# Another cut of one output stream into store slots (pairwise products, one core)

## The chip, the cores and the metric

One core of a Trainium2 chip runs the whole kernel. The metric is the device time of one execution in microseconds (us); the time of a kernel is the median of its runs.

## The reference, cut to what matters

```python
def _L0_rec_ref(x, W):                          # x (4096, 32, 64), W (64, 64), float32
    vid = jnp.einsum('bfd,de->bfe', x, W)
    idx_i, idx_j = jnp.triu_indices(32, k=1)    # 496 pairs i < j
    return x[:, idx_i, :] * vid[:, idx_j, :]    # (4096, 496, 64)
```

Each of 4096 samples has 32 fields of 64 numbers. The fields are multiplied by one 64x64 matrix, and for each of the 496 pairs (i, j) the field i is multiplied, element by element, with the transformed field j. The input has 33.6 MB, the output 520.1 MB.

## The kernel before, in words

**Layout.** The 128 partitions hold two halves of the batch times the 64 embedding numbers. The batch of one half is cut into 16 tiles of C = 128 samples. A **unit** is one field or one pair of one tile: 128 partitions by 128 float32, 64 KB. A tile has 32 units of input and 496 units of output; the program writes 16 * 496 = 7936 units of output, in one long row. The host brings the arrays into this layout and back.

**Memory.** The SBUF tile `mem` has 445 units. Everything lies in it: the inputs of the tiles (at `XPLACE`) and the products that wait to be stored. PSUM holds `vid`, the 32 transformed fields of one tile.

**Work on one tile.** TensorE multiplies the tile with the matrix into `vid` (L173, in pieces of 4 fields). VectorE then forms the products (L197): one `tensor_tensor` multiplies several left fields with several right fields and writes a run of units (112 at most) that lie one behind the other in the output. `by_block` gives the order of the runs. Left operands come from `mem`, right ones from PSUM.

**Slots.** The row of 7936 output units is cut into slots by the list `SLOTS`. A slot is (number of units, place in `mem`, seams...). At most 127 units are in a slot. When the products of a slot are done, one DMA stores it (L200). `STARTS` are the ends of the slots in the output row; `BREAKS` are these ends and the seams inside the slots. The function `products` splits a run of products wherever a break lies in it, so every break inside a run costs more VectorE instructions. A seam is put where the place of a slot crosses the edge of an older slot whose store may still be on its way: the products ahead of the seam need not wait for that store.

**What waits for what.** A product waits for the matmuls of its right fields, for the load of its tile, and for every older store (or load) whose place in `mem` it writes over. A matmul waits until VectorE has read the old contents of its part of `vid`. A store waits for the products of its slot. The first store behind a group of loads also waits until the last but one piece of these loads has landed (`behind`). All DMAs are issued by SP and go through one queue.

**Order.** Only SP keeps the order of the program text (`manual_schedule` with SP alone). The order of the instructions on VectorE and TensorE is set when the kernel is built, by the scheduler of the framework; it mostly follows the text, but it may put a ready product ahead of others. Loads are three groups: tile 0 to 5 at the start, tiles 6 to 10 at about 382 us, tiles 11 to 15 at about 790 us (L152).

Of the kernel before, what the change touches and what calls it, by code (L numbers as in the profile page):

```python
# [26 lines left out]


SLOTS = [
    (108, 80), (116, 201), (96, 64, 16), (96, 161, 40), (60, 257), (108, 64, 97), (92, 172),  # L30
    (84, 265), (127, 80, 92), (127, 222, 43), (98, 64, 16), (92, 162, 60), (127, 254), (120, 64),
    (124, 184, 70), (104, 308), (124, 112, 72), (124, 240), (124, 64, 48), (124, 192, 48),
    (124, 317), (124, 152, 40), (96, 64, 88), (124, 161), (112, 32, 32), (85, 144, 17), (56, 229),
    (104, 48), (116, 160, 69), (127, 1, 47), (72, 128, 32), (85, 200), (124, 32), (127, 160, 40),
    (85, 0, 32), (118, 85, 75), (114, 203), (127, 32, 53), (127, 159, 44), (123, 0, 32),
    (123, 123, 36), (127, 246), (112, 0), (127, 119), (126, 246), (127, 160, 86), (124, 289),
    (88, 160), (81, 248, 41), (84, 329), (104, 160, 88), (92, 264, 65), (88, 357), (127, 176, 88),
    (127, 318, 39), (127, 136, 40), (127, 272, 46), (94, 128), (106, 222, 50), (116, 328),
    (127, 160, 62), (127, 288, 40), (127, 120, 40), (127, 247, 41), (127, 64, 56), (124, 191, 56),
    (124, 317), (127, 32), (127, 160), (124, 289), (103, 136, 24),  # L40
]


# [210 lines left out]
```

## Time and profile before

| | |
|---|---|
| median of 3 runs | 1288.05 us (1287.6 to 1288.36) |
| the profiled execution | 1287.84 us, of which the span from the first to the last instruction is 1286.1 us |
| moved by DMA | 553.79 MB, mean 431 GB/s over the span |
| VectorE busy | 1091.1 us, 456 instructions |
| TensorE busy | 223.2 us, 512 matmuls in the trace |
| stores | 71, of at most 127 units (8128 KB) |

The page gives the busy time of each engine, the span in 40 slices, the DMA queues, the chain of work that ended last, the groups of instructions with their mean durations, and the DMA issues with the time from issue to landing. "SPq" is the queue of SP: the time that its next DMA stood waiting. Beside the page the trace has the record of each DMA packet (start, duration, size) and of each instruction.

### The profile page before, as it was taken

Reading aid. Unit: us, or ns where it says so; the run is one execution under the profiler, and the core shown is the slowest. Engines: PE = TensorE matmul, PEld = TensorE weight load, DVE = VectorE, ACT = ScalarE, POOL = GpSimd, SP = SyncE. Lnnn points to the kernel's source line nnn. Section 1 sums busy time; section 2 is a strip of 40 time slices with the busy share of each in tenths; the row PEclk is TensorE's granted clock in tenths of the full one; section 3 lists DMA queues with packets and bytes.
Section 4 is the critical chain, followed back from the end, with each engine's and each line's share of the span. In section 5 each row is a group of like instructions: output and inputs, shape, how many; then the busy total and the mean of one; then the engine's idle time right before and its main releaser. Section 6 shows DMA issues by size and latency. Waiting matters only on the chain.

```text
span 1286.1 us, 1762 instructions
## 1 busy us (share of the span) xinstructions
PE 223.2 (17%) x512; PEld 41.0 (3%) x512; DVE 1091.1 (85%) x456; POOL 0.2 (0%) x4
## 2 busy tenths in 40 slices
PE   4031221303120113030311311103131130312000
PEld 1000000000000000000000000000000000000000
DVE  6899889988995489998998995649999799999952
POOL 0000000000000000000000000000000000000000
PEclk8565555555555655555555555555555565656555
DMA  9999999999999999999999999999999999999998
GB/s 415 434 422 429 434 447 425 437 433 440 415 440 419 445 426 427 436 423 435 444 432 424 442 422 445 421 423 434 436 441 431 421 437 433 441 431 433 428 441 380
DMA packets 11817, 553.79 MB, mean 431 GB/s; under 512 B 1312, under 2 KB 1312, under 8 KB 1696
## 3 DMA queue, kind: packets, MB, share of 16 engines
q1 hardware_dynamic: 11808, 553.69, 99.8%
q8 instruction: 4, 0.07, 0.0%
q14 instruction: 5, 0.04, 0.0%
HBM read 33.59 MB, written 520.09 MB: 431 GB/s over the span
## 4 chain that ended last, share of the span: by engine, by line
DMA 51%; DVE 44%; issue 3%; PE 0%; DVEq 0%; SPq 0%
DVE mem L197 44%; DMA out_dram<-mem 44%; DMA mem<-in_r_x_dram 7%; PE vid L173 0%; DVEq L242 0%; SPq L152 0%; SPq L200 0%; DVEq L197 0%; DVE w L142 0%
## 5 line engine op out<-in xcount | busy, mean ns | idle before, releaser
L197 DVE TENSOR_TENSOR mem<-mem,vid 128x1024 f32<-128x1024 f32 (+16 forms) x455 | 1090.9, 2471 | 164.9 <-DMA out_dram<-mem 154.8
L173 PE MATMUL vid<-mem,w 64*64 64x512 f32 x512 | 223.2, 996 | 961.0 <-DVE mem L197 863.5
L173 PEld LDWEIGHTS vid<-mem,w 64*64 64x64 f32 x512 | 41.0, 198 | 1141.6 <-DVE mem L197 1007.7
L142 DVE COPY w<-mem 128x64 f32<-128x64 f32 x1 | 0.2, 195 | 5.8 <-DMA mem<-in_r_x_dram 5.8
L222 POOL MEMSET const-uint8-127<- 128x1 uint8 x1 | 0.1, 102 | 0.0
L222 POOL MEMSET const-bfloat16-1.0<- 128x1 bf16 x1 | 0.1, 101 | 0.0
L222 POOL MEMSET const-float32-0.0<- 128x1 f32 x1 | 0.1, 98 | 0.2 <-issue 0.2
L222 POOL MEMSET const-float32-1.0<- 128x1 f32 x1 | 0.1, 98 | 0.0
## 6 DMA issues: line engine op xcount, KB each, us to landing
out_dram<-mem SPq DMA_DIRECT2D x21, 8128.0 KB, 26.7
out_dram<-mem SPq DMA_DIRECT2D x13, 7936.0 KB, 28.2
out_dram<-mem SPq DMA_DIRECT2D x3, 7424.0 KB, 24.2
out_dram<-mem SPq DMA_DIRECT2D x3, 6656.0 KB, 22.7
out_dram<-mem SPq DMA_DIRECT2D x3, 6144.0 KB, 20.9
out_dram<-mem SPq DMA_DIRECT2D x3, 5888.0 KB, 23.9
out_dram<-mem SPq DMA_DIRECT2D x3, 5440.0 KB, 24.6
mem<-in_r_x_dram SPq DMA_DIRECT2D x2, 8128.0 KB, 39.2
```

Source lines behind the costliest of these rows:

```text
L142: nc.vector.tensor_copy(w2, mem[:, place - 1, C - D :])
L173: nc.tensor.matmul(vid[half, b : b + BANK, :], lhsT=w2[half, :], rhs=xt[half, b : b + BANK, :], start=True, stop=True,)
L197: nc.vector.tensor_tensor(o, left, right, ALU.mult)
L222: nc = _bacc.Bacc("TRN2", target_bir_lowering=False, num_devices=1, dynamic_dma_scratch_size=1024)
```

## The change

The list `SLOTS` is another one. Nothing else is changed.

```diff
 SLOTS = [
-    (108, 80), (116, 201), (96, 64, 16), (96, 161, 40), (60, 257), (108, 64, 97), (92, 172),
-    (84, 265), (127, 80, 92), (127, 222, 43), (98, 64, 16), (92, 162, 60), (127, 254), (120, 64),
-    (124, 184, 70), (104, 308), (124, 112, 72), (124, 240), (124, 64, 48), (124, 192, 48),
-    (124, 317), (124, 152, 40), (96, 64, 88), (124, 161), (112, 32, 32), (85, 144, 17), (56, 229),
-    (104, 48), (116, 160, 69), (127, 1, 47), (72, 128, 32), (85, 200), (124, 32), (127, 160, 40),
-    (85, 0, 32), (118, 85, 75), (114, 203), (127, 32, 53), (127, 159, 44), (123, 0, 32),
-    (123, 123, 36), (127, 246), (112, 0), (127, 119), (126, 246), (127, 160, 86), (124, 289),
-    (88, 160), (81, 248, 41), (84, 329), (104, 160, 88), (92, 264, 65), (88, 357), (127, 176, 88),
-    (127, 318, 39), (127, 136, 40), (127, 272, 46), (94, 128), (106, 222, 50), (116, 328),
-    (127, 160, 62), (127, 288, 40), (127, 120, 40), (127, 247, 41), (127, 64, 56), (124, 191, 56),
-    (124, 317), (127, 32), (127, 160), (124, 289), (103, 136, 24),
+    (96, 221), (120, 80), (116, 200, 21), (100, 64, 16), (92, 164, 36), (92, 256), (127, 96, 68),
+    (124, 223, 33), (125, 64), (120, 191), (64, 311), (112, 79), (124, 224), (108, 64),
+    (120, 176, 48), (112, 301), (120, 64), (112, 205), (120, 320), (112, 93), (127, 205), (121, 64),
+    (96, 189), (120, 48), (116, 168, 21), (100, 32), (104, 132, 36), (48, 236), (124, 16),
+    (127, 157, 79), (109, 0, 16), (120, 109, 48), (88, 229), (127, 16, 93), (127, 160, 69),
+    (114, 0, 16), (120, 114), (112, 237), (127, 0), (121, 128), (120, 261), (127, 1), (127, 128),
+    (122, 259), (120, 176), (116, 297), (92, 160, 16), (88, 252, 45), (72, 341), (120, 160, 92),
+    (120, 293, 48), (32, 413), (120, 173), (126, 319), (122, 144), (127, 287, 32), (119, 128, 16),
+    (126, 247), (127, 96), (109, 223), (112, 333), (127, 158), (127, 285), (127, 64, 94),
+    (127, 192, 93), (124, 320), (120, 48), (127, 190), (124, 317), (125, 158),
 ]
```

There are 70 slots with 22 seams in place of 71 with 41, and VectorE has 345 products in place of 455. The list is one line shorter, so L197 of before is L196 of the changed kernel, and so on.

As built, the changed kernel has its VectorE products in the order of the program text, but for two of them. One of 4 units stands four places early (in the slot (92, 160, 16)). The other is one of 80 units of the slot (127, 64, 94), which stands five places early. This is the part of the built order with it; "n units at p" is a product of n units that is written to place p of `mem`, and the slot that it belongs to stands behind it:

```
96 at 236                                          (109, 223)   waits for the store of (126, 247)
112 at 333                                         (112, 333)
16 at 158, 8 at 174, 8 at 182, 8 at 190, 16 at 198 (127, 158)   the first waits for the store of (127, 96)
16 at 214, 48 at 230, 7 at 278                     (127, 158)   the first waits for the store of (109, 223)
1 at 285, 8 at 286, 8 at 294, 8 at 302, 8 at 310   (127, 285)
80 at 66                                           (127, 64, 94)   <- in the text behind the next five
16 at 318, 16 at 334, 56 at 350, 6 at 406          (127, 285)   the first waits for the store of (112, 333)
2 at 64, 12 at 146, ...                            (127, 64, 94)
```

In the kernel before, products stand ahead of their place in the text too, eleven groups of them, the largest product among them of 16 units.

## The prediction

> **What bounds the kernel now.** I read the page from its totals downward. First the busy times beside the DMA rows:
>
> ```profile
> PE 223.2 (17%) x512; PEld 41.0 (3%) x512; DVE 1091.1 (85%) x456; POOL 0.2 (0%) x4
> DMA  9999999999999999999999999999999999999998
> DMA packets 11817, 553.79 MB, mean 431 GB/s; under 512 B 1312, under 2 KB 1312, under 8 KB 1696
> q1 hardware_dynamic: 11808, 553.69, 99.8%
> ```
>
> The 16 DMA engines are busy for 99.8% of the span, in every slice; VectorE for 85%. So the kernel is a stream of DMA, and its time is the bytes by the rate, plus the start, plus every microsecond in which the DMA engines have nothing to do. The packet records agree: from the first store on, all 16 engines have a packet in flight practically always. The bytes are the same after the change, so it can gain next to nothing from VectorE's time. The question is only whether a store comes too late.
>
> Then the waits, VectorE's and SP's own:
>
> ```profile
> DVE mem L197 <- DMA out_dram<-mem: 154.8, 34, 22.7
> SPq L200 <- DVE mem L197: 1100.8, 66, 33.6
> ```
>
> It is a ring. VectorE waits for room in `mem` (34 times, until a store has landed); SP waits for VectorE before 66 of its stores. The memory is so full that hardly more than one finished store stands behind the running one. How much is in hand is read from the chain of waits, whose DMA pieces run from a store's issue to its landing:
>
> ```profile
> 588.41 23.26 DMA out_dram<-mem
> ...
> 1053.72 24.57 DMA out_dram<-mem
> ...
> 1129.96 26.09 DMA out_dram<-mem
> ```
>
> The first and third are stores of 127 units, the second one of 116. By the packet records 127 units alone take 19.2 us and 116 units 17.6 us, so these stood some 4 to 7 us, landing included. The records of the first packets give the cover itself, issue to first packet: 2.0 us for the store at 588.41 (the smallest inside a group of tiles), 4.6 to 7 us for most. A store issued to idle engines (at 30.70) needs 0.84 us to its first packet. So cover beyond 0.84 us is what VectorE may be late.
>
> [...]
>
> **The price of a product.** From the groups kept apart by shape:
>
> ```profile
> L197 DVE TENSOR_TENSOR mem<-mem,vid 128x8192 f32<-128x8192 f32 x28 | 243.0, 8679 | 7.0 <-DMA out_dram<-mem 7.0
> L197 DVE TENSOR_TENSOR mem<-mem,vid 128x2048 f32<-128x2048 f32 x71 | 160.0, 2278 | 1.1 <-DMA out_dram<-mem 1.1
> L197 DVE TENSOR_TENSOR mem<-mem,vid 128x10240 f32<-128x10240 f32 x5 | 54.0, 10811 | 0.0
> ```
>
> (8679 - 2278) / (8192 - 2048) = 1.0418 ns for each element, so one unit (128 elements) costs 0.1333 us, and 2278 - 2048 * 1.0418 leaves 144 ns for the instruction. Neighbours overlap: in the trace a product that waits for nothing starts 80 ns before the end of the one ahead. One more split thus costs 144 - 80 = 65 ns. A unit in the DMA queue costs 65,536 B / 433 GB/s = 0.1514 us (127 of them: 19.2 us). VectorE is quicker by 0.018 us a unit, 2.3 us for a store of 127; it regains cover at that pace and then waits for room.
>
> **The change part by part.**
> - *110 products fewer.* 110 * 65 ns = 7.2 us less of VectorE's work over the whole kernel. It lies beside DMA that is busy 99.8% of the time: gain on the path 0. The bound on the other side is the idle DMA time that exists, 0.2% of 1286 us = 2.6 us, most of it the start and end, which stay.
> - *One store fewer, other sizes.* The packets' durations (2401 ns for 65,024 B, 1062 ns for 28,672 B) leave about 6 ns for each packet beyond the bytes, 8 packets of a store on each engine: 0.05 to 0.1 us gained. SP's issue (0.33 us each) is hidden behind the running store.
> - *First and last slot.* The first store still waits for the load pieces, as at 30.70 now. The last store is 125 units and not 103; it is queued behind a running one in both. The loads have the same pieces; only the stores that they wait for differ. I take 0 for these; bounds -0.5 and +0.5 us.
> - *The order on VectorE.* This is the part that counts. As built, a product of 80 units for (127, 64, 94) stands in front of the last 94 units of (127, 285). The store of (127, 285) waits for it, and SP's queue has nothing else to send: the next store is (127, 64, 94) itself.
>
> I lay the stretch out from the landing of the store (126, 247), for which VectorE waits. From there to the end of (127, 285) it works off 96 + 112 + 127 + 127 + 80 = 542 units in 1 + 1 + 8 + 9 + 1 = 20 products: 542 * 0.1333 + 20 * 0.065 = 73.6 us. Between a store's end on an average engine and the next product, and from product to next packet, the records give 0.55 (the slowest engine ends later), 0.5 (landing to product) and 0.84 to 0.9 (issue to packet): 2.0 us in all. So 75.6 us must be covered. What DMA has to do from the end of (126, 247) is (127, 96), (109, 223), (112, 333), (127, 158): 475 * 0.1514 = 71.9 us. DMA stands idle for **3.7 us**. Without the 80 units early (80 * 0.1333 + 0.065 = 10.7 us) it would have 7.0 us in hand. A count from the later landing of (109, 223) gives the same 3.7 us, so two waits lead to it.
>
> I walked the other 69 stores with these prices, and the kernel before as well. In the kernel before no store comes late, and the walk's issue times stay within about 1.5 us of the trace; its smallest cover inside a group is 3.3 us where the trace has 2.0. In the changed kernel this store (issued near 1135 us) is the only late one; the next smallest covers are 3.7 to 4.6 us, some 2.8 us above need. The late 3.7 us can't be regained, for DMA runs at its rate before and after; all that follows moves by it.
>
> Sum: 1287.84 (the profiled execution: span 1286.1 and 1.7 around it) + 3.7 - 0.1 = 1291.4 us; the median of the runs stands 0.2 above the profiled one, so 1291.7 us.
>
> Bounds of the idle time: the spread between DMA engines is 0.3 to 2 us in the records. With 0.2 for the lateness of the slowest engine the walk gives 3.4 us, with 1.5 it gives 4.7. Against it, a stop lines up all engines, and what the slow ones lag at the end (0.7 us now) may be less: down to 2.7 us.
>
> **The rivals.**
> - *The cover holds (not slower).* One mechanism: the product of 80 units is absorbed by stores still queued. The 0.2 us by which VectorE's waits vary can't do it; the backlog at the landing of (126, 247) would have to be larger by 24 units of DMA, or the turnaround of 2.0 us shorter. It decides from 1.2 us: with the idle time under 2.5 us the result is no change, at 3.7 us less it is 1288.0 us. For it: slow packets (up to 3.7 us in the records) delay the running stores now and then and let VectorE catch up. Against: they then delay the landings too, for which VectorE waits.
> - *More than one store runs dry.* The cover of many stores is 4.1 to 4.6 us by the walk, which stood up to 1.3 us above the trace. If a slow packet takes 3 us more in one place, 1 to 3 us are added: 1294 us.
> - *The DMA gets quicker.* With fewer VectorE instructions and one store fewer, the most that 99.8% leaves is 2.6 us: 1285.5 us. Nothing in the page speaks for it.
>
> **How the numbers follow.** 0.2% is 2.6 us, about what a measurement of this kernel can tell from no change. The late store: 0.80, at 1291.7 us. The cover holds in good part: 0.13. More stores dry: 0.05. Quicker: 0.02. The range is 1289.3 to 1293.6 us: the late store with its bounds (2.7 to 4.7 us), half of the partial cover below, and one more short stop above. The chance of slower by more than 0.2% is that of the late store (less a small part under 2.6 us) and of more stores dry, 0.83; the same 0.15; faster 0.02.
>
> **What would show it.** In the trace after: VectorE with some 345 products and about 1084 us busy; in the chain and in SP's waits a store issued near 1135 us some 28 us after the one before; its way from issue to landing only about 20.5 us, its own 19.2 us and no queue; a DMA slice near 1135 us at a lower rate; no other store under 1 us of cover. It is wrong if that store has more than 0.84 us from issue to first packet, if VectorE's order differs, or if time is lost or gained away from 1135 us.

## The result, and the profile after

The changed kernel takes 1290.92 us (median of 12 runs, 1290.44 to 1291.36), the kernel before 1287.98 us (12 runs beside it, 1287.6 to 1288.36). The ratio is 1.0022, with a 95% interval of 1.0013 to 1.0031: slower by 2.9 us, where 3.7 us were forecast. The profiled execution took 1290.48 us with a span of 1288.7 us, 2.6 us longer than before.

The page after, totals, DMA rows and the group of the products:

```profile
PE 219.6 (17%) x512; PEld 42.2 (3%) x512; DVE 1084.0 (84%) x346; POOL 0.2 (0%) x4
DMA  9999999999999999999999999999999999989999
GB/s 416 432 423 439 443 436 423 434 424 443 420 453 411 422 435 431 443 439 430 423 442 427 433 443 430 423 418 432 447 433 418 441 440 418 448 361 452 435 414 412
DMA packets 11672, 553.78 MB, mean 430 GB/s; under 512 B 1296, under 2 KB 1296, under 8 KB 1680
q1 hardware_dynamic: 11664, 553.69, 99.6%
L196 DVE TENSOR_TENSOR mem<-mem,vid 128x1024 f32<-128x1024 f32 (+16 forms) x345 | 1083.8, 3213 | 173.6 <-DMA out_dram<-mem 168.1
```

VectorE lost 7.1 us of work (1091.1 to 1084.0), and the kernel became slower. The bytes of queue q1 are the same 553.69 MB, its share fell from 99.8 to 99.6%. One digit of the DMA row is an 8 now, and the same slice, number 36 of 40, has 361 GB/s with its neighbours at 448 and 452. A slice is 32.2 us, so this is 1127.6 to 1159.8 us.

The waits after, VectorE's and SP's:

```profile
DVE mem L196 <- DMA out_dram<-mem: 168.1, 37, 20.8
SPq L199 <- DVE mem L196: 1101.2, 66, 33.4
```

SP's total hardly moved. VectorE's wait is 13.3 us longer (154.8 before), and most of that is 7.1 us less of work and a run longer by 2.6 us. Neither total points at a place. The chain of waits around that slice does:

```profile
1061.31 0.06 DVE mem L196
...
1109.09 25.89 DVE mem L196 x8
1134.98 20.59 DMA out_dram<-mem
1155.57 0.02 issue
...
1160.44 33.64 DMA out_dram<-mem
```

From the landing of (126, 247), behind which VectorE starts at 1061.31, the chain has no DMA piece for 73.7 us. The timeline shows that VectorE works through all of it without a wait (its line goes on past the late store, to 1154 us):

```profile
1061.31 92.83 DVE L196 TENSOR_TENSOR mem<-mem,vid 128x12288 f32<-128x12288 f32 x28 [3.73 <-DMA out_dram<-mem]
```

Then comes a DMA piece of 20.59 us: the store of (127, 285), issued at 1134.98. That is 0.83 us to its first packet, its own 19.4 us and the landing, and no queue. The issue ahead of it was at 1106.74, 28.2 us earlier. The store of the same size that the prediction shows from the chain of before has 26.09 us, 4.6 us of them from issue to first packet; the next one here has 33.64. By the packet records the last engine had finished at 1133.56 and the first packet of the late store started at 1135.81. As a mean over the 16 engines, each stood idle for 3.81 us between 1130 and 1140 us.

### The profile page after: what moved, and what is told of

It is laid out like the page before. It is cut to its first block, busy times and chain, and to the rows that moved or that the text cites. A ratio compares the mean times of both kernels' runs of the same rounds, so it can differ in the third digit from the quotient of the medians.

```text
span 1288.7 us, 1651 instructions
## 1 busy us (share of the span) xinstructions
PE 219.6 (17%) x512; PEld 42.2 (3%) x512; DVE 1084.0 (84%) x346; POOL 0.2 (0%) x4
## 3 DMA queue, kind: packets, MB, share of 16 engines
q1 hardware_dynamic: 11664, 553.69, 99.6%
## 4 chain that ended last, share of the span: by engine, by line
DMA 50%; DVE 42%; issue 6%; DVEq 0%; SPq 0%
DMA out_dram<-mem 45%; DVE mem L196 42%; DMA mem<-in_r_x_dram 5%; DVEq L241 0%; SPq L151 0%; DVEq L196 0%; SPq L140 0%; SPq L136 0%; SPq L199 0%
## 5 line engine op out<-in xcount | busy, mean ns | idle before, releaser
L196 DVE TENSOR_TENSOR mem<-mem,vid 128x1024 f32<-128x1024 f32 (+16 forms) x345 | 1083.8, 3213 | 173.6 <-DMA out_dram<-mem 168.1
L172 PE MATMUL vid<-mem,w 64*64 64x512 f32 x512 | 219.6, 988 | 961.1 <-DVE mem L196 853.3
```

Source lines behind the costliest of these rows:

```text
L172: nc.tensor.matmul(vid[half, b : b + BANK, :], lhsT=w2[half, :], rhs=xt[half, b : b + BANK, :], start=True, stop=True,)
L196: nc.vector.tensor_tensor(o, left, right, ALU.mult)
```

## The experiments

"Idle" is the time without a packet in flight, a mean over the 16 DMA engines, counted from the packet records of the profiled execution: in the middle (the stop), and at the end, from the first engine that has nothing more to do until the last one is through. "Cover" is issue to first packet of the store of (127, 285), in e7_early_stop too, where the stop is at another store. The times are medians.

| kernel | us | before on the same chip | idle, stop | idle, end | cover |
|---|---|---|---|---|---|
| before | 1287.98 | | 0 | 1.16 | |
| after | 1290.92 | 1287.98 | 3.81 | 0.08 | 0.83 |
| e1_text_order | 1288.09 | 1288.29 | 0 | 1.14 | 3.59 |
| e2_hand_early | 1291.06 | 1288.29 | 3.83 | 0.09 | 0.83 |
| e3_early_48 | 1288.24 | 1287.97 | 0 | 1.16 | 1.03 |
| e3b_early_64 | 1288.98 | 1287.97 | 1.69 | 0.11 | 0.83 |
| e6_early_94 | 1292.95 | 1287.97 | 5.83 | under 0.08 | 0.83 |
| e4_more_splits | 1288.15 | 1288.29 | 0 | 1.18 | 5.61 |
| e7_early_stop | 1291.34 | 1288.29 | 3.87 (at 520 us) | 1.07 | 4.03 |
| e5_before_text_order | 1288.25 | 1287.97 | 0 | 1.16 | |

**e1_text_order: the new slots, VectorE in the order of the text.**

```diff
-    ctx.enter_context(tc.manual_schedule(engines={mybir.EngineType.SP}))
+    ctx.enter_context(tc.manual_schedule(engines={mybir.EngineType.SP, mybir.EngineType.DVE}))
```

> The slots of the changed kernel, VectorE held to the order of the program text (the product of 80 units stands behind the last 94 units of (127, 285) again). Theory (the early product makes one store late): the store of (127, 285) is issued near 1124 us with some 7 us of cover, no DMA engine stands idle in the middle, and the median is 1287.9 us (1287.5 to 1288.3), that of the kernel before. Rival (the new slots cost time by their sizes and places, whatever the order): 1290.9 us stays.

Measured: 1288.09 us (13 runs), ratio to the kernel before 0.9998 (0.9990 to 1.0007). The whole loss is gone, and the slots are the same. So the slots as such cost nothing; the order on VectorE that came with them does. One detail was missed: the store is issued at 1128.25 us with 3.6 us of cover, not at 1124 with 7. The timeline of this kernel, VectorE and the stores, says why:

```profile
1106.86 56.36 SPq L199 DMA_DIRECT2D out_dram<-mem  x4
1115.34 50.38 DVE L196 TENSOR_TENSOR mem<-mem,vid 128x2048 f32<-128x2048 f32 x19 [3.78 <-DMA out_dram<-mem]
```

In the order of the text VectorE has to wait 3.78 us for the landing of (112, 333) before it can go on with (127, 285). In the changed kernel the product of 80 units stands in this wait. VectorE gains 3.8 us that nobody needs, and the store of (127, 285) is 6.7 us later (1128.25 to 1134.98), on the path. Part of the wait is a late landing: (112, 333) landed 1.72 us after its last packet's end, while the other stores of this execution needed 0.3 to 0.5 us.

**e2_hand_early: e1_text_order, and the product of 80 units put early by hand.** The products of a tile go through a function that moves one of them; `ROWS` is empty here, and splits the product in the next two kernels.

```diff
+MOVES = [(7064, 6968)]      # the product at output unit 7064 goes ahead of the one at 6968
+ROWS = {}
+def placed(todo):
...
+    for at, ahead in MOVES:
+        for k, p in enumerate(out):
+            if p[0] == at:
+                part = out.pop(k)
+                out.insert([p[0] for p in out].index(ahead), part)
+                break
+    return out
...
-        for at, m, w, i, di, j, dj in products(by_block(), t * NP):
+        for at, m, w, i, di, j, dj in placed(products(by_block(), t * NP)):
```

> As e1_text_order, but the product of 80 units is put early by hand, five places ahead, where the scheduler had it. Theory: the loss comes back whole, DMA engines stand idle some 3.8 us near 1134 us, median 1290.9 us. Rival (holding VectorE to the text changes something else, and that was the gain): it stays where e1_text_order is.

Measured: 1291.06 us (12 runs), ratio 1.0022 (1.0014 to 1.0031), the changed kernel over again. Its chain has the same piece:

```profile
1109.65 25.90 DVE mem L218 x8
1135.55 20.59 DMA out_dram<-mem
```

One product, five places away from its own, makes the whole difference.

**e3_early_48, e3b_early_64, e6_early_94: how much stands early.**

```diff
-ROWS = {}
+ROWS = {7064: 3}            # e3: 48 units early; {7064: 4} in e3b: 64 units
...
-MOVES = [(7064, 6968)]
+MOVES = [(7064, 6968), (7062, 6968), (7144, 6968)]      # e6: 94 units
```

> As e2_hand_early, but only the first 3 rows (48 units) of the product of 80 units stand early; the other 32 units stand behind, so VectorE has 346 products. Theory (the loss is what is over the cover): 48 units are 6.5 us against some 7 us of cover, the store is issued just in time (0.9 to 1.4 us of cover left), idle time at most 0.3 us, median 1288.1 us as in e1_text_order. Rival (any product put early costs about its own share or a fixed sum): 1289.5 to 1291 us.

> As e3_early_48 with 4 rows (64 units) early: 8.6 us. Theory: DMA engines stand idle 1.6 to 2.0 us near 1133 us; since a late stop gave about 0.9 us back at the end in the changed kernel, the median is 1288.7 to 1289.4 us. Rival (a fixed sum for a late store): 1291 us.

> As e2_hand_early, with the two products around it (2 units at 64, 12 units at 146) put early too, so 94 units stand early: 12.7 us. Theory: idle 5.7 to 5.9 us near 1137 us, 2 us more than in e2_hand_early, median 1293.0 us (1292.6 to 1293.4). Rival (a fixed sum): 1291 us.

Measured: 1288.24, 1288.98 and 1292.95 us (13, 13 and 5 runs; ratios 1.0002, 1.0008 and 1.0038, with 95% intervals of 0.9993 to 1.0010, 1.0000 to 1.0016 and 1.0025 to 1.0050). A fixed sum is out. Below the cover nothing is lost: with 48 units early the store has 1.03 us from issue to first packet, 0.2 more than the 0.83 us of the stores that found the queue idle. Above it the stop grows at VectorE's price: 1.69, 3.81 and 5.83 us for 64, 80 and 94 units. From 64 to 94 that is 4.14 us for 30 units and two instructions, where the prices give 30 * 0.1333 + 2 * 0.065 = 4.13. The early products of 8.6, 10.7 and 12.7 us less these stops leave 6.9 us each time: that is the room. The chain of e6_early_94:

```profile
1109.87 27.87 DVE mem L218 x9
1137.74 0.02 issue
1137.76 20.60 DMA out_dram<-mem
```

**e4_more_splits: e1_text_order with 110 needless breaks.**

```diff
+MORE = [...]                # 110 places between two rows of a run, spread over the whole output
-BREAKS = sorted({a + s for a, (_, _, *seams) in zip(STARTS, SLOTS) for s in seams} | set(STARTS))
+BREAKS = sorted(set(MORE) | {a + s for a, (_, _, *seams) in zip(STARTS, SLOTS) for s in seams} | set(STARTS))
```

> As e1_text_order, with 110 needless breaks inside runs, so that VectorE has 455 products again. Theory (VectorE's instructions lie beside a busy DMA): VectorE is busy 7.2 us more (1091 us), and the median doesn't move: 1287.9 us, within 0.5 of e1_text_order. Rival (products are time on the path): up to 7.2 us more, 1295 us.

Measured: 1288.15 us (13 runs), 0.06 us from e1_text_order. The totals of its page, with those of e1_text_order below:

```profile
PE 224.8 (17%) x512; PEld 40.4 (3%) x512; DVE 1091.0 (85%) x456; POOL 0.2 (0%) x4
```

```profile
PE 218.8 (17%) x512; PEld 42.1 (3%) x512; DVE 1083.8 (84%) x346; POOL 0.2 (0%) x4
```

110 products are 7.2 us of VectorE, 65 ns each, and no time of the kernel.

**e7_early_stop: a stop of the same kind in the first half.**

```diff
+REPEAT = {3048: 2}
...
-            nc.vector.tensor_tensor(o, left, right, ALU.mult)
+            for _ in range(REPEAT.get(at, 1)):
+                nc.vector.tensor_tensor(o, left, right, ALU.mult)
```

> As e1_text_order, and the product of 48 units at the start of the slot (124, 16) is done twice, which makes that store 6.5 us later (near 521 us). By the walk over the stores DMA stands idle 3.1 to 3.7 us there. Theory (a stop late in the kernel gives about 1 us back, since it lines up DMA engines of which one would end 1.1 us behind the others; after an early stop they drift apart again): here the whole stop is lost, 1291.0 to 1291.6 us, and at the end the engines are apart by about 1 us on average again. Rival (a stop anywhere costs 1 us less than its idle time): 1290.0 to 1290.6 us.

Measured: 1291.34 us (9 runs), ratio 1.0024 (1.0015 to 1.0034). Its chain shows the stop, a store of 124 units (19.0 us of its own) without a queue:

```profile
521.84 0.02 issue
521.86 20.16 DMA out_dram<-mem
```

This kernel was to tell whether the engines part again after a stop, and the records say yes. The spread between the first engine to take up a store and the last one to end the store ahead is 2.0 us at 497 us, 0.1 at 560 us, 0.8 at 628, 1.8 at 888 and 1.6 at 1231 us. The larger steps are at about 577 us and across the loads that follow at 805 us; no loads follow the late stop of the other kernels. At the end 1.07 us are idle again. The page shows the end of a kernel with and without a late stop in its last two slices of GB/s. After has 414 and 412; here it is 439 and 386:

```profile
GB/s 414 418 437 439 442 428 430 434 424 443 429 443 411 420 436 426 388 442 428 428 439 442 412 441 444 416 422 432 443 431 442 438 429 432 437 430 426 435 439 386
```

In the profiled execution the span is 3.7 us longer than in e1_text_order (1289.6 to 1285.9), for 3.7 us more of idle time altogether. In the medians it is 3.25 us, and only 0.28 us more than the late stop of e2_hand_early, where the idle times of the two profiles differ by 0.9. Two thirds of what an early stop should cost over a late one are missing there. The engines' own busy time differs from execution to execution by some 0.8 us (a mean of 1282.8 us here, 1283.6 in e2_hand_early), and the profile shows one execution of each. So the profiles show that the engines part again, but how much of the early stop's price comes from that stays open.

**e5_before_text_order: the kernel before, VectorE in the order of the text.** The edit is that of e1_text_order, in the kernel before.

> The kernel before (its 71 slots), VectorE held to the order of the program text; eleven groups of early products go back to their places. Theory (the early products of before are 16 units at most and lie under the cover): the smallest cover inside a group rises from 2.0 us to over 3.5 us, and the time stays at 1288.1 us, within 0.4 of the kernel before. Rival (the scheduler's order is worth something by itself, for it fills VectorE's waits): slower by 1 us or more.

Measured: 1288.25 us (13 runs), ratio 1.0002 (0.9994 to 1.0011). No store inside a group of tiles has under 4.2 us of cover; before, the smallest was 2.0. The early products of the kernel before cost cover and no time, and they bring none.

## Why the prediction was right, point by point

- **The bound.** It is the DMA stream: q1 is at 99.6 to 99.8% in after and e1_text_order, and the engines' own busy time is 1283.1 us as a mean over the 16, before and after. Between these two profiles the idle time alone differs: 2.67 us more in all, for a span longer by 2.6.
- **110 products fewer: 0.** Right. VectorE has 1084.0 us where 1083.9 follow from the step, and e4_more_splits puts the 7.2 us back without effect.
- **One store fewer, first and last slot: about 0.** e1_text_order has both and stands 0.2 us under the kernel before, inside the interval. Not told apart from 0.
- **The late store.** Right in place, mechanism and size. The sum put the issue near 1135 us (1134.98), the queue at 0.84 us (0.83) and the stop at 3.7 us (3.81). Its terms hold one by one: 73.7 us of products (73.6), 2.0 us of turnaround (1.19 from the mean end of (126, 247) to VectorE's start, and 0.83), and 71.95 us of stores ahead (71.9). The 433 GB/s that prices a unit in the queue is what before moved from 1075 to 1150 us, with stores alone and a DMA share of 1.00. e1, e2 and the three sizes show the cause: it is the product of 80 units, by what it exceeds the room in front of that store.
- **The 0.84 us of an idle queue.** Right as a figure, and partly by luck. It was read from the store at 30.70, but there all 16 engines still had packets of the last load in flight until 31.4 us, so that store does not show an idle queue. The late stores do, with 0.83 us.
- **"7.0 us in hand" without the early product.** Wrong as a statement on the text's order, where VectorE waits 3.78 us for (112, 333) and the cover is 3.59 us, 2.8 us more than the 0.83. The step left this wait out. The prediction's own prices give, as an estimate, 348 * 0.1514 - (368 * 0.1333 + 15 * 0.065) = 2.7 us for it, and e7_early_stop waits 2.41 us at this place; the rest in e1_text_order is the late landing. The figure is right as the room that an early product may take (6.9 us), since that wait passes in the meantime: 48 units (6.5 us) just fit.
- **The only late store.** Right. The next smallest cover inside a group is 3.0 us, at 515 us, where the walk had nothing under 3.7. The first stores behind the loads have 0.84 to 0.88 us, as they had 0.84 to 0.95 before, and the last piece of the loads is still running there: the engines stand idle for under 0.1 us.
- **The 3.7 us all reach the end.** This is the term that was mis-sized: 2.9 us arrived. The bounds named a cause ("a stop lines up all engines"; in after the engines end the store ahead of the stop 1.88 us apart, and the late store 0.16 us) and put the lag at the end at 0.7 us, but the sum gave it nothing. Before, 1.16 us of idle time lie at the end, because one or a few engines lag (the last one ends 0.75 us behind the next); after, 0.08. 3.81 - 1.08 = 2.73 agrees with the span's 2.6 us and with the median's 2.9. All four kernels with a late stop end with at most 0.11 us idle there, all those with none or an early one with 1.07 to 1.18. So the profiles account for the missing part; that it is the whole reason is not shown, because the early stop of e7_early_stop keeps its 1.07 us at the end and costs only 0.28 us more in the medians.
- **The rivals.** "The cover holds" did not occur at 80 units, but is what e3_early_48 does at 48. More dry stores: none. A quicker DMA: the packets' median for 65,024 B is 2404 ns after and 2401 ns before.

On the price of a split: a product that waits for nothing starts 80 ns before the end of the one ahead, the median in before and in after. With this overlap a split costs 65 ns (144 - 80), as the 110 splits of e4_more_splits show with their 7.2 us.

## What to carry to other kernels

When the DMA queue is the bound, as it is here at 99.6 to 99.8%, count a change on another engine by one question: when is each store issued, and how much is queued then. Here 110 instructions more on a VectorE that is 84 to 85% busy moved the time by 0.06 us, while one product of 80 units that the scheduler moved ahead of the last products of a store left the DMA engines idle for 3.81 us. So compare the built order, not only the source, and look for a store whose time from issue to landing is its bare transfer (here 20.59 us, 19.4 of them its own).

## What the runs showed of the hardware that was not expected

- A store is 128 packets of one size, by count 8 for each of the 16 DMA engines, and still the engines part. In before and after they end a transfer 0.4 to 0.9 us apart in the first 110 us and up to 2.0 us apart later. Single packets of 56 to 64 KB took 2.7 to 3.7 us there, where the median for 65,024 B is 2.40. Of 39 such packets in after, 30 lie where the queue goes over from stores to loads (402 and 805 us), some elsewhere (149 us). Packets over 0.15 us above the median of their size add 2.7 us for each engine in before and 2.6 in after, as a mean. The last store's end is that of the slowest engine, and the others were idle there for 1.07 to 1.18 us on average; in the four kernels with a stop at about 1135 us it is at most 0.11 us.
- With the queue idle, a store had 0.83 us from its issue to its first packet, in each of the five kernels with a late store.
- The stores landed 0.3 to 0.5 us after their last packet's end, but one store in each of seven of the ten profiled executions landed 1.7 to 1.8 us after it. With the new slots that is (112, 333), in all runs but e4_more_splits and e7_early_stop. In these runs one packet of that store was slow too (2.7 us in place of 2.12). The reason stays open.
